# Self-attention projections: which batch stores the split weight slices, and when the first slices are loaded

## The chip, the core and the metric

The kernel runs on one core of a Trainium2 chip. The core has TensorE (PE, matrix products into PSUM; PEld is its loading of weights), VectorE (DVE), ScalarE (ACT), GpSimd (POOL) and SyncE (SP). SP issues most DMAs, ACT a few; both queues are served in order, so a DMA that must wait holds up all that stand behind it. The metric is the device time of one execution in microseconds (us). Several runs are taken and the median counts.

## What is computed

A decoder layer on four sequences (batches 0 to 3) of 1024 tokens with 512 features, followed by a gated fusion. Only the first third matters here, causal self-attention with 16 heads of 32 features:

```python
xn1 = _ln(x, g1, be1)
q = jnp.einsum('btc,hcd->bhtd', xn, Wq) + bq[None, :, None, :]
k = jnp.einsum('bsc,hcd->bhsd', kv_src, Wk) + bk[None, :, None, :]
v = jnp.einsum('bsc,hcd->bhsd', kv_src, Wv) + bv[None, :, None, :]
scores = jnp.einsum('bhtd,bhsd->bhts', q, k) / scale     # scale = DH ** (-0.5)
attn = jax.nn.softmax(jnp.where(mask, scores, -jnp.inf), axis=-1)
out = jnp.einsum('bhts,bhsd->bhtd', attn, v)
x = x + (sa @ W1 + b1)
...                       # cross-attention, feed-forward, gated fusion
```

The scores are large (divided by a number below 1), so products are made with more than one pass of PE: every operand is held as a high part and a low part (the rest after rounding), and three products are added, high x high, high x low, low x high.

## The kernel before, in words

**Phases.** `self_attention`, `cross_attention` and `feed_forward` follow one another. Only the first is touched.

**Units and pieces.** A batch has four head groups g (four heads, 128 features) and two token halves n of 512. A *piece* `project(b, n, g)` makes k and q of one group and half: two times twelve matmuls of 128x512 (`pk`, `pq`), each started by a step `load` that fetches the weight slice of 128 columns if n is 0. `values(b, n, half)` makes v for half of the features: four times twelve matmuls of 128x256 (`pv`), with a slice of 256 columns. `front(b, n)` loads four blocks of x (L524), normalises them (`stats_s`, `mv_s`, `rstd_s`, then L178), transposes them on PE (`tpn_s`, L534) and splits them into `xn` (L74 the high half on ACT, L75 the low one on DVE).

The results of k, q and v go to DRAM (L623 `kd<-k`, `qd<-q`; L594 `vd<-vout`) and come back rearranged as *stacks* of three parts (L646 `ks<-kd`, `qs<-qd`; L668 `v<-vd`). A *unit* u is one group and half of the query tiles; units are numbered through the batches. `maxima(u)` makes the scores of a unit (L692 `s<-ks,qs`), takes row maxima on DVE (L699 and L702, results `least` and `top`), transposes them (`tpm`) and writes them as extra rows of the query stack (L732 `qs<-mT`). `attend(u)` makes the scores again with that row included (L755 `st`), takes the exponential on ACT (L760), sums on POOL and DVE (L809) and multiplies with v (L785 `av`).

**Weight slices.** `weight_slice` is called for each slice (k and q: i = 0 to 3, v: i = 0 and 1) in each batch. In batch 0 it loads the raw slice into the one buffer `stage` (L577 `st_k`, `st_q`, `st_v`; 256 KB, v 512 KB), makes the high half on ACT (L578) and the low half on DVE (L579), and stores both halves to DRAM (L581 `wk<-wk`, 512 KB, v 1 MB). In batches 1 to 3 it loads the two halves from there (L569). Slices of k and q have four buffers, those of v one.

**What sets the order.** `run` merges streams of steps by their weights (main, ahead, fill); a timeline planner then orders the instructions of each engine at build time, by the cost it gives each of them. `tc.issue_after(i)` keeps what follows behind instruction i in that order; `behind(engine)` does so for the last instruction of an engine. `ones_rows` fills four rows of the key stacks by memsets on POOL (L510). While unit u is attended, the stream `ahead` holds the maxima of the next units, and `fill` the projections of unit u + 4.

Of the kernel before, what the change touches and what calls it, by code (L numbers as in the profile page):

```python
# [10 lines left out]
F32 = mybir.dt.float32  # L11
FR = mybir.dt.float32r
# [6 lines left out]
P = 128  # L19
B, T, C, H = 4, 1024, 512, 16  # L20
# [3 lines left out]
NC = C // P  # L24
NF = FF // P
TG = 512
# [20 lines left out]
def raw(ap):  # L47

    return ap.bitcast(F32)
# [3 lines left out]
def decoder_then_fusion(ctx: ExitStack, tc: tile.TileContext, x, ctxT, cols, rows,  # L53
                        Wq_s, Wk_s, Wv_s, W1, Wq_c, Wk_c, Wv_c, W2, Wf1, Wf2,
                        Wt, WvT, WgT, out):
    nc = tc.nc
# [34 lines left out]
    def product_steps(psum_of, a, b, a_at, b_at, width, end, bias=None):  # L91


        held = {}

        def step(c):
            if c == 0:
                held["ps"] = psum_of()
                if bias:
                    nc.tensor.matmul(held["ps"], *bias(), start=True, stop=False)  # L100
            for k, (i, j) in enumerate(((0, 0), (0, 1), (1, 0))):
                nc.tensor.matmul(held["ps"], a_at(a()[i], c), b_at(b()[j], c),  # L102
                                 start=not bias and c == 0 and k == 0, stop=c == NC - 1 and k == 2)
            if c == NC - 1:
                end(held["ps"])

        per = Z["per"]

        def steps(c):
            for i in range(c, c + per):  # L110
                step(i)

        return [(3 * width * per, lambda c=c: steps(c)) for c in range(0, NC, per)]
# [48 lines left out]
    latest = {}  # L162
# [290 lines left out]
    def self_attention(ph):  # L453
# [62 lines left out]
        def front(b, n):  # L516

            uid = f"s{b}_{n}"
            hs = []

            def load(j):
                i = n * NJ + j
                t = xp.tile([P, C], F32, tag="x", name=f"x_{b}_{i}")
                nc.sync.dma_start(t, x[b, i * P : (i + 1) * P, :])  # L524
                normalise(t, t, f"{uid}_{j}")
                hs.append(t)

            def turn(c):
                if c == 0:
                    xn[b, n] = [xnp.tile([P, NC, TG], FR, tag=f"xn{n}_{k}", name=f"xn{k}_{uid}") for k in range(2)]  # L530
                parts = xn[b, n]
                tp = psum(f"tpn_{uid}_{c}")
                for j, t in enumerate(hs):
                    nc.tensor.transpose(tp[:, j * P : (j + 1) * P], t[:, c * P : (c + 1) * P], ident)  # L534
                with tc.issue_after(latest["hi"]) if c and (b, n) in Z["chain"] else ExitStack():
                    nc.scalar.activation(tp, tp, AF.Identity, bias=col("be1", c), scale=col("g1", c))
                split(parts[0][:, c, :], parts[1][:, c, :], tp, f"{uid}_{c}")

            return [(0, lambda j=j: load(j)) for j in range(NJ)], [(TG, lambda c=c: turn(c)) for c in range(NC)]
# [19 lines left out]
            return slice(at[0] * P, (at[-1] + 1) * P), slice(first * P, (first + len(at)) * P)  # L559


        sources = {"k": (Wk_s, 1.0), "q": (Wq_s, -1.0), "v": (Wv_s, 1.0)}
        slices = {}

        def weight_slice(which, i, w):

            t = wp.tile([P, 2, NC, w], FR, tag=f"w{w}", name=f"w{which}_{i}", bufs=None if w == P else 1)
            if (which, i) in slices:
                nc.sync.dma_start(raw(t), slices[which, i])  # L569
                return t  # L570
            src, sign = sources[which]
            if Z["wst"]:
                st = wp.tile([P, 2 * TG], F32, tag="stage", name=f"st_{which}_{i}", bufs=Z["wst"])
            else:
                st = ptp.tile([P, 2, TG], F32, tag="pT", name=f"st_{which}_{i}").rearrange("p a b -> p (a b)")
            st = st[:, : NC * w].rearrange("p (c n) -> p c n", c=NC)
            nc.sync.dma_start(st, chunks(src)[:, :, i * w : (i + 1) * w])  # L577
            nc.scalar.activation(t[:, 0], st, AF.Copy, scale=sign)  # L578
            nc.vector.scalar_tensor_tensor(t[:, 1], st, sign, t[:, 0], ALU.mult, ALU.subtract)  # L579
            slices[which, i] = dram.tile([P, 2, NC, w], F32, tag=f"w{which}{i}", name=f"w{which}{i}")  # L580
            nc.sync.dma_start(slices[which, i], raw(t))  # L581
            return t

        ws = {}

        def values(b, n, half):
            def load():
                if n == 0:
                    ws["v"] = weight_slice("v", half, C // 2)

            def end(ps, j):
                v = outp.tile([P, C // 2], F32, tag="vout", name=f"vout_{b}_{n}_{half}_{j}")
                nc.scalar.copy(v, ps)
                nc.sync.dma_start(v_dram[b,][:, n * NJ + j, half * (C // 2) : (half + 1) * (C // 2)], v)  # L594

            steps = [(0, load)]
            for j in range(NJ):
                steps += product_steps(
                    lambda j=j: psum(f"pv_{b}_{n}_{half}_{j}")[:, : C // 2],
                    lambda: xn[b, n], lambda: [ws["v"][:, 0], ws["v"][:, 1]],  # L600
                    lambda a, c, j=j: a[:, c, j * P : (j + 1) * P], lambda w, c: w[:, c, :], C // 2,
                    lambda ps, j=j: end(ps, j))
            return steps

        def project(b, n, g):
            steps = []
            for which, to in (("k", k_dram), ("q", q_dram)):
                def load(which=which):
                    if n == 0:
                        ws[which, g] = weight_slice(which, g, P)  # L610

                def end(ps, which=which, to=to):
                    parts = [qkp.tile([P, TG], FR, tag=f"part{k}", name=f"{which}{k}_{b}_{n}_{g}")
                             for k in range(2)]
                    bias = col("bk_s", g) if which == "k" else nbq[:, g : g + 1]
                    split_biased(parts[0], parts[1], ps, bias)

                    moves = [(to[b, n, g], slice(0, TG), slice(0, TG))] if which == "k" else [
                        (to[b, h, g], *shared) for h, tiles in enumerate(tiles_of(b, g))
                        if (shared := columns(tiles, n))]  # L620
                    for dram_tile, at, src in moves:
                        for k in range(2):
                            nc.sync.dma_start(dram_tile[k][:, at], raw(parts[k])[:, src])  # L623

                steps.append((0, load))
                steps += product_steps(
                    lambda which=which: psum(f"p{which}_{b}_{n}_{g}"),
                    lambda which=which: [ws[which, g][:, 0], ws[which, g][:, 1]], lambda: xn[b, n],
                    lambda a, c: a[:, c, :], lambda a, c: a[:, c, :], TG, end)
            return steps  # L630
# [10 lines left out]
        def pile(stack, src, parts):  # L641

            for i, k in enumerate(parts):
                nc.sync.dma_start(raw(stack)[i * DH : (i + 1) * DH], src[k].rearrange("(r d) t -> d r t", d=DH))  # L646

        def load_stacks(u, since):

# [22 lines left out]
        def maxima(u):  # L672
# [12 lines left out]
            def scores(blocks):  # L685
# [3 lines left out]
                for r, j, m in blocks:  # L689
                    part = sc[:, at : at + width(tiles[j], m)]  # L690
                    at += width(tiles[j], m)
                    nc.tensor.matmul(part, q_at[u][:KS, r, j * P : (j + 1) * P],  # L692
                                     k_at[u, m][:KS, r, : part.shape[-1]], start=True, stop=True)
                    parts.append(part)
                for part, (r, j, m) in zip(parts, blocks):
                    far = tiles[j] >= NJ
# [159 lines left out]
        for b, g, n in [(b, g, n) for b in range(B) for g in range(NC) for n in range(NG)]:  # L856
            piece = project(b, n, g)
            if (g, n) == (0, 0):
                piece = ((among(piece, fronts[b, 1][1]) if Z["amt"] else fronts[b, 1][1] + piece) if b else
                         fronts[b, 0][0] + [(0, ones_rows)] + fronts[b, 0][1] + fronts[b, 1][0] + piece  # L860
                         + fronts[b, 1][1] + values(b, 0, 0))
            elif (g, n) in Z["val"]:
                piece = piece + values(b, *Z["val"][g, n])
            if b + 1 < B:
# [74 lines left out]
        for u in range(len(units)):  # L939
# [17 lines left out]
            if u >= first_late:  # L957
                fill, part = [], Z["late"][u - first_late] * total
                while rest and (part > 0 or u + 1 == len(units)):
                    part -= rest[0][0]  # L960
                    fill.append(rest.pop(0))
            else:
                fill = pieces[u + AHEAD]
            run(main, ahead, fill, speed=(Z["main"], (Z["ahead%d" % n] if u < Z["alf"] else Z["ahead_l"]) if u else Z["a0"], Z["fill"]), sooner=(Z["so0"], Z["so1"], Z["so2"]))
        first, others, end = tail()
        first()
# [840 lines left out]
```

## Time and profile before

| | |
|---|---|
| median of 3 runs | 2146.06 us (2144.63 to 2152.42) |
| profiled execution | 2153.24 us, span 2151.5 us |
| mean granted clock of PE | 0.983 |
| PE busy | 2064.3 us, 96% of the span |
| DVE, ACT, POOL busy | 1452.1 (67%), 967.5 (45%), 1210.7 us (56%) |
| moved by DMA | 379.36 MB, mean 176 GB/s |
| first weight slice loaded and split | 2.6 to 8.7 us |
| first scores (L692) | 37.2 us |
| self-attention | up to about 880 us |

The profile is that of one execution. In the tables of stretches each engine has its busy time and its number of instructions; PEclk is the clock that was granted to PE, as a share of the full one, and DMA share the mean busy share of the core's 16 DMA engines. A line "A <- B: t, n, m" of the waits says that A waited for B t us in n waits, the longest of m us. The chain of waits lists, in order of time, the start, the length and the name of each link of the chain that ended last; for a DMA this is from issue to landing. In a timeline, a line has start, busy time, engine, source line and operation, result and operand, and how many were merged.

### The profile page before, as it was taken

Reading aid. Unit: us, or ns where it says so; the run is one execution under the profiler, and the core shown is the slowest. Engines: PE = TensorE matmul, PEld = TensorE weight load, DVE = VectorE, ACT = ScalarE, POOL = GpSimd, SP = SyncE. Lnnn points to the kernel's source line nnn. Section 1 sums busy time; section 2 is a strip of 40 time slices with the busy share of each in tenths; the row PEclk is TensorE's granted clock in tenths of the full one; section 3 lists DMA queues with packets and bytes.
Section 4 is the critical chain, followed back from the end, with each engine's and each line's share of the span. In section 5 each row is a group of like instructions: output and inputs, shape, how many; then the busy total and the mean of one; then the engine's idle time right before and its main releaser. Section 6 shows DMA issues by size and latency. Waiting matters only on the chain.

```text
span 2151.5 us, 34750 instructions
## 1 busy us (share of the span) xinstructions
PE 2064.3 (96%) x11544; PEld 1568.7 (73%) x11544; DVE 1452.1 (67%) x3134; ACT 967.5 (45%) x2180; POOL 1210.7 (56%) x1257
## 2 busy tenths in 40 slices
PE   6999998999999989989999999999999999999997
PEld 5766676667667756457888887788788888888885
DVE  6587757665755587567676776877667846865667
ACT  3365555555565545435555557433322422232222
POOL 3288878888788877774555543512343524433323
PEclk9999999999999998999999999999999999999998
DMA  8866767677666567662323122965576457655631
GB/s 245 258 186 168 218 203 216 182 243 219 190 174 186 158 171 213 206 204 79 99 84 103 50 79 86 332 210 170 182 238 198 166 175 237 207 175 171 220 113 39
DMA packets 241321, 379.36 MB, mean 176 GB/s; under 512 B 35948, under 2 KB 104284, under 8 KB 239094
## 3 DMA queue, kind: packets, MB, share of 16 engines
q1 hardware_dynamic: 215532, 348.32, 52.4%
q10 hardware_dynamic: 25610, 28.83, 4.4%
q8 instruction: 92, 1.51, 0.3%
q14 instruction: 87, 0.71, 0.1%
HBM read 251.71 MB, written 124.81 MB: 175 GB/s over the span
## 4 chain that ended last, share of the span: by engine, by line
PE 76%; DMA 7%; DVE 7%; POOL 4%; issue 2%; ACT 1%; SPq 1%; ACTq 0%; DVEq 0%; POOLq 0%
PE acc L1495 15%; PE ph L1473 14%; PE st L755 5%; PE s L692 5%; PE av L785 5%; PE po_c L102 4%; PE pq_x L102 3%; PE pk L102 3%; PE pv L102 3%; PE pg_o L102 3%; PE po_x L102 3%; PE pq L102 3%; POOL pT L809 2%; PE sc_c L87 2%; PE av_c L1139 1%
## 5 line engine op out<-in xcount | busy, mean ns | idle before, releaser
L809 POOL TENSOR_TENSOR pT<-pT,pT 128x256 f32<-128x256 f32 (+3 forms) x369 | 551.6, 1514 | 106.0 <-PE av L785 97.1
L760 ACT ACTIVATE pT<-st 128x512 f32<-128x512 f32 (+2 forms) x640 | 322.3, 559 | 171.2 <-PE st L755 122.9
L1495 PE MATMUL acc<-wf,hs 128*128 128x512 f32 x1536 | 392.1, 393 | 0.9 <-DVE y L1507 0.9
L1495 PEld LDWEIGHTS acc<-wf,hs 128*128 128x128 f32 x1536 | 285.8, 188 | 63.1 <-ACT inT L74 1.3
L699 DVE CUSTOM_DVE_ANT_0 s<-s,mask 128x128 f32<-128x128 f32 (+3 forms) x512 | 244.5, 504 | 99.6 <-PE s L692 97.1
L692 PE MATMUL s<-ks,qs 96*128 96x512 f32 (+3 forms) x768 | 230.2, 371 | 23.0 <-DMA qs<-qd 7.3
L702 DVE TENSOR_REDUCE top<-s 128x1 f32<-128x512 f32 x256 | 171.9, 684 | 104.4 <-PE s L692 103.9
L755 PE MATMUL st<-qs,ks 98*128 98x256 f32 (+2 forms) x888 | 227.8, 340 | 4.7 <-ACT pT L760 2.0
L1473 PE MATMUL ph<-inT,wp 128*128 128x512 f32 x768 | 205.3, 396 | 3.1 <-DVE p L1431 1.2
L755 PEld LDWEIGHTS st<-qs,ks 98*128 98x128 f32 x888 | 149.4, 192 | 63.7 <-issue 20.2
L692 PEld LDWEIGHTS s<-ks,qs 96*128 96x128 f32 x768 | 135.6, 194 | 81.0 <-issue 17.0
L1473 PEld LDWEIGHTS ph<-inT,wp 128*128 128x128 f32 x768 | 143.9, 189 | 36.6 <-DVE gp_o L1568 1.8
L785 PE MATMUL av<-pT,v 128*32 128x512 f32 (+3 forms) x1776 | 155.1, 454 | 4.1 <-POOL pT L768 4.1
L1473 PE MATMUL ph<-inX,wp 128*128 128x512 f32 x576 | 151.4, 395 | 1.1 <-DVE inX L75 1.1
L768 POOL TENSOR_SCALAR_AFFINE_SELECT pT<-pT 128x256 f32<-128x256 f32 x256 | 103.7, 421 | 73.6 <-ACT pT L760 73.1
L1473 PEld LDWEIGHTS ph<-inX,wp 128*128 128x128 f32 x576 | 108.4, 189 | 25.2 <-issue 1.3
L1542 POOL TENSOR_TENSOR y<-y,row_bf 128x512 f32<-128x512 f32 x32 | 41.6, 1304 | 132.6 <-DMA y<-x 72.1
L1481 ACT ACTIVATE hs<-ph 128x512 fp32r<-128x512 f32 x64 | 38.3, 599 | 172.2 <-DVE ph L1431 99.4
L102 PE MATMUL pk<-xn_s,wk 128*128 128x512 f32 x384 | 106.1, 412 | 4.9 <-DVE top L702 3.0
L102 PE MATMUL pv<-wv,xn_s 128*128 128x256 f32 x768 | 108.1, 286 | 2.5 <-DVE least L699 1.6
L102 PEld LDWEIGHTS pv<-wv,xn_s 128*128 128x128 f32 x768 | 102.1, 192 | 11.4 <-DVE top L699 2.9
L1118 POOL TENSOR_TENSOR p_c<-p_c,inv_c 128x512 f32<-128x512 f32 x64 | 68.4, 1069 | 73.9 <-DVE inv_c L1117 58.6
(262 smaller groups left out, 3907.8 us busy)
## 6 DMA issues: line engine op xcount, KB each, us to landing
wp<-wpd SPq DMA_DIRECT2D x168, 256.0 KB
ks<-kd SPq DMA_DIRECT2D x96, 256.0 KB
qs<-qd SPq DMA_DIRECT2D x96, 256.0 KB
wf<-w2fd SPq DMA_DIRECT2D x48, 512.0 KB
kd<-k SPq DMA_DIRECT2D x64, 256.0 KB
qd<-q SPq DMA_DIRECT2D x120, 128.0 KB
wpd<-wp SPq DMA_DIRECT2D x56, 256.0 KB
x<-in_x SPq DMA_DIRECT2D x32, 256.0 KB
```

The source lines that it names most:

```text
L102: nc.tensor.matmul(held["ps"], a_at(a()[i], c), b_at(b()[j], c), start=not bias and c == 0 and k == 0, stop=c == NC - 1 and k == 2)
L692: nc.tensor.matmul(part, q_at[u][:KS, r, j * P : (j + 1) * P], k_at[u, m][:KS, r, : part.shape[-1]], start=True, stop=True)
L699: nc.vector.tensor_tensor_reduce(part, part, mask[:, TG - part.shape[-1] :], 1.0, TOP, ALU.add, ALU.min, dst)
L702: nc.vector.tensor_reduce(dst, part, AX.X, ALU.min)
L755: nc.tensor.matmul(st[:, i], k_at[u, kb // NJ][:KM, r + i, (kb % NJ) * P : (kb % NJ + 1) * P], q_at[u][:KM, r + i, c0:], start=True, stop= ...
L760: nc.scalar.activation(held[kb][(r + i) // 2][:, at : at + k, c0:], st[:, i : i + k], AF.Exp, scale=-QSCALE)
L768: nc.gpsimd.affine_select(out=t, in_=t, compare_op=ALU.is_ge, fill=0.0, base=0, pattern=[[0, 2], [1, P]], channel_multiplier=-1)
L785: return nc.tensor.matmul(held["av"][r * DH : (r + 1) * DH, c0:], v_at[b, g][:, kb, r * DH : (r + 1) * DH], held[kb][r // 2][:, r % 2, c0: ...
L809: eng.tensor_tensor(t[:, :, c0:], t[:, :, c0:], p[:, :, c0:], ALU.add)
L1118: nc.gpsimd.tensor_tensor(pr, pr, inv.unsqueeze(2).to_broadcast([P, HH, S]), ALU.mult)
L1473: nc.tensor.matmul(ps, w[:, q, c], x[:, r, c], start=c == 0 and m == 0, stop=c == HC - 1 and m == 2)
L1495: mm = nc.tensor.matmul(accs[j], hidden[b, n, f][:, q, j * P : (j + 1) * P], w2s[b, f][:, r], start=begins and m == 0, stop=ends and m == 2)
```

## The change

- Slices are made per batch. In batch 0 they are split and not stored. In batch 1 (`b == True` holds for b = 1, as `LATER` names all slices) the raw slices are loaded and split once more and stored. Batches 2 and 3 load the stored halves as before.
- The first slices of k and q of batch 0 are loaded into two free `pT` buffers (2 of the 7 that hold exponentials later), by steps that come right after the first four loads of x. All other raw slices share the one `stage` buffer, as before.
- The memsets of `ones_rows` come after the loads and the normalisation of the second half.
- Batch 1's loads of x wait, in SP's order, for the last instruction that SP has been given so far.
- The score matmuls of unit 1 wait, in PE's order, for the latest projection matmul; and during unit 0 the stream `ahead` begins with an empty step of weight 4 x 512.

```diff
@@ product_steps @@
             for k, (i, j) in enumerate(((0, 0), (0, 1), (1, 0))):
-                nc.tensor.matmul(held["ps"], a_at(a()[i], c), b_at(b()[j], c),
-                                 start=not bias and c == 0 and k == 0, stop=c == NC - 1 and k == 2)
+                latest["product"] = nc.tensor.matmul(
+                    held["ps"], a_at(a()[i], c), b_at(b()[j], c),
+                    start=not bias and c == 0 and k == 0, stop=c == NC - 1 and k == 2).ins
@@ front @@
-                nc.sync.dma_start(t, x[b, i * P : (i + 1) * P, :])
+                with behind(nc.sync) if b == 1 else ExitStack():
+                    nc.sync.dma_start(t, x[b, i * P : (i + 1) * P, :])
@@ slices @@
+        LATER = [(w, i) for w in 'kqv' for i in range(NC)]
+        FIRST = ((0, 0, "k"), (0, 0, "q"))
+
+        def first_slices():
+            def load(which):
+                ws[which, 0] = weight_slice(0, which, 0, P)
+            return [(0, lambda which=which: load(which)) for _, _, which in FIRST]
+
-        def weight_slice(which, i, w):
+        def weight_slice(b, which, i, w):
...
-            if Z["wst"]:
-                st = wp.tile([P, 2 * TG], F32, tag="stage", name=f"st_{which}_{i}", bufs=Z["wst"])
+            if (b, i, which) not in FIRST:
+                st = wp.tile([P, 2 * TG], F32, tag="stage", name=f"st_{which}_{b}_{i}", bufs=1)
             else:
                 st = ptp.tile([P, 2, TG], F32, tag="pT", name=f"st_{which}_{i}").rearrange("p a b -> p (a b)")
...
-            slices[which, i] = dram.tile([P, 2, NC, w], F32, tag=f"w{which}{i}", name=f"w{which}{i}")
-            nc.sync.dma_start(slices[which, i], raw(t))
+            if b == ((which, i) in LATER):
+                slices[which, i] = dram.tile([P, 2, NC, w], F32, tag=f"w{which}{i}", name=f"w{which}{i}")
+                nc.sync.dma_start(slices[which, i], raw(t))
@@ values, project @@
-                    ws["v"] = weight_slice("v", half, C // 2)
+                    ws["v"] = weight_slice(b, "v", half, C // 2)
-                    if n == 0:
-                        ws[which, g] = weight_slice(which, g, P)
+                    if n == 0 and (b, g) != (0, 0):
+                        ws[which, g] = weight_slice(b, which, g, P)
@@ maxima @@
+        def among_fill():
+            return tc.issue_after(latest["product"])
...
-                    nc.tensor.matmul(part, q_at[u][:KS, r, j * P : (j + 1) * P],
-                                     k_at[u, m][:KS, r, : part.shape[-1]], start=True, stop=True)
+                    with among_fill() if u == 1 else ExitStack():
+                        nc.tensor.matmul(part, q_at[u][:KS, r, j * P : (j + 1) * P],
+                                         k_at[u, m][:KS, r, : part.shape[-1]], start=True, stop=True)
@@ the pieces of (g, n) == (0, 0), batch 0 @@
-                         fronts[b, 0][0] + [(0, ones_rows)] + fronts[b, 0][1] + fronts[b, 1][0] + piece
-                         + fronts[b, 1][1] + values(b, 0, 0))
+                         fronts[b, 0][0] + first_slices() + fronts[b, 0][1] + fronts[b, 1][0]
+                         + [(0, ones_rows)] + piece + fronts[b, 1][1] + values(b, 0, 0))
@@ the loop over units @@
+            if u == 0:
+                ahead.insert(0, (4 * TG, lambda: None))
             run(main, ahead, fill, ...)
```

The names and line numbers in the prediction are those of the kernel before.

More of the change, by code (lines that the diff above doesn't have):

```diff
@@ L559, in columns @@
             return slice(at[0] * P, (at[-1] + 1) * P), slice(first * P, (first + len(at)) * P)
+        LATER = [(w, i) for w in 'kqv' for i in range(NC)]
         sources = {"k": (Wk_s, 1.0), "q": (Wq_s, -1.0), "v": (Wv_s, 1.0)}
         slices = {}
-        def weight_slice(which, i, w):
-            t = wp.tile([P, 2, NC, w], FR, tag=f"w{w}", name=f"w{which}_{i}", bufs=None if w == P else 1)
+        FIRST = ((0, 0, "k"), (0, 0, "q"))
[4 more added lines that the diff above has]
+        def weight_slice(b, which, i, w):
+            t = wp.tile([P, 2, NC, w], FR, tag=f"w{w}", name=f"w{which}_{b}_{i}", bufs=None if w == P else 1)
             if (which, i) in slices:
```

## The prediction

> **What bounds the kernel now.** I began with the table of busy time by stretch, cut where the orders of instructions of the two kernels differ: every engine's order has changed from the start until about 645 us, and from there on it is the same.
>
> ```profile
> core 0: us, PE busy (x) PEld busy (x) DVE busy (x) ACT busy (x) POOL busy (x), PEclk, DMA share, GB/s
> 0.00:67.00 67.00, 47.75 (x226) 37.77 (x227) 40.89 (x100) 22.33 (x38) 20.20 (x41) 0.92 0.78 237
> ...
> 100.00:180.00 80.00, 77.59 (x507) 52.68 (x506) 66.15 (x169) 47.12 (x94) 61.59 (x62) 1.00 0.69 195
> 180.00:340.00 160.00, 156.53 (x1071) 112.51 (x1070) 101.32 (x305) 89.34 (x179) 132.82 (x135) 1.00 0.70 201
> 340.00:400.00 60.00, 54.40 (x347) 38.06 (x345) 37.70 (x108) 32.20 (x64) 46.71 (x52) 0.91 0.56 169
> ```
>
> PE sets the pace: 97% busy from 100 to 340 us. Time can be won only where it stands or is slow, and that is the opening: 19.25 of the first 67 us idle, at a mean clock of 0.92, with the DMA engines at 78% (99% from 20 to 40 us). Next, what PE waited for up to 160 us (total, times, longest):
>
> ```profile
> PE tpn_s L534 <- DVE x L178: 8.4, 3, 6.8
> PE s L692 <- DMA qs<-qd: 5.1, 2, 3.1
> PE s L692 <- DVE top L702: 1.7, 2, 0.9
> PE pv L102 <- DVE least L699: 1.6, 1, 1.6
> PE tpm L726 <- DVE least L699: 1.4, 1, 1.4
> ```
>
> The first line is the wait for the first activations (6.8 at the start), which the change leaves. The rest is stack loads and VectorE's score maxima. The chain of waits dates them:
>
> ```profile
> 28.93 8.26 DMA qs<-qd
> 37.23 0.55 PE s L692 x2
> 37.78 2.41 PE pk L102 x6
> ...
> 48.26 7.93 DMA qs<-qd
> ...
> 57.19 4.92 PE pk L102 x12
> ```
>
> Each stack load of 256 KB takes 8 us to land, PE stands before both (1.94 and 3.13 us), and the projection after each runs at about half speed: 0.40 us a matmul, against 0.23 for the twelve at 92.96 (2.75 us). Last, SP's queue between 25 and 33 us, in order:
>
> ```profile
> 25.33 0.34 SPq L581 DMA_DIRECT2D wv<-wv  x1
> 25.76 0.38 SPq L646 DMA_DIRECT2D ks<-kd  x1
> 26.19 3.55 SPq L646 DMA_DIRECT2D qs<-qd  x3
> 29.78 0.51 SPq L594 DMA_DIRECT2D vd<-vout  x1
> 30.33 0.49 SPq L577 DMA_DIRECT2D st_k<-in_Wk_s  x1
> 30.92 2.00 SPq L524 DMA_DIRECT2D x<-in_x  x2
> ```
>
> A store of 1 MB (wv) goes out just ahead of the stacks that PE waits for, and batch 1's activations just after.
>
> **The change, part by part.** *Stores removed from batch 0:* eight of 512 KB and two of 1 MB, 6 MB. *In batch 1* ten loads of split slices (6 MB) become ten raw loads (3 MB) with a split each and ten stores (6 MB). The splits are 8 x 0.63 + 2 x 1.06 = 7.2 us more on ACT and 8 x 0.69 + 2 x 1.22 = 8.0 on DVE. *Moved:* the raw loads of the first k, q and v slices go ahead of x_4; those of k 1, q 1 and v 1 ahead of the first k and q stores; batch 1's four x loads and their statistics from 31-50 us to behind unit 1's loads, which the new order puts at 110-170 us; four memsets of POOL (1.8 us each, 9.6 to 16.9) behind the second half's rstd; unit 1's first scores behind twelve matmuls of pk_0_1.
>
> I follow PE by landmarks.
>
> *Start of the projections: loses 1.5 us, 0 to 2.6.* DVE's first low half (13.64) gets wv's split and two statistics more ahead of it: 1.22 + 2 x 0.69 = 2.6. Against that, x_2 and x_3 took 2.11 us together beside the memsets, where x_0 and x_1 took 0.5 each; with the memsets gone, 1.0 comes back.
>
> *First scores: 2.5 us earlier, start included; -3 to +4.* Slices of k 1, q 1 and v 1 share one stage buffer, so each load waits on SP for the split before it, and the stores of the first k and q are queued behind all three; ACT's copy of k, too, stands behind q 1's split. From 13.5 us (wv split) two rounds of load, ACT and DVE follow. A raw load took 3.5 us (103.49) to 7.7 (30.33, in the crowd); I take 4, since little else is in flight: 13.5 + 2 x (4 + 1.3) = 24.1, where kd goes out at 21.88 now. So the store is 2.2 us later. But 17.8 to 37.2 us carries 4736 KB now and 3456 KB afterwards (no wq and wv stores, a q load instead); 1.3 MB at 295 GB/s are 4.4 us. The stacks land at about 34.5 instead of 37.23. With 7.7 us a load they land after 40.
>
> *First scores to the maxima's transpose (37.2 to 52.9): 3 us, 1.5 to 4.5.* DVE loses four statistics and four normalisations of batch 1 (4 x (0.69 + 0.17 + 0.55) = 5.6) and two splits here. PE's three waits for it (1.63, 0.45, 1.44) mostly go, and the six slow matmuls (2.41 against 1.38) are warm.
>
> *Unit 1's scores: 4 us, 2 to 5.3.* Their stacks get no wk, wq or x traffic beside them, but two vout stores stand ahead of qs on SP. The 3.13 us wait is covered by pk_0_1 (2.75 us), which needs only k 1, long split. Its cold clock costs 4.92 - 2.75 = 2.17 now. All is 5.3; I keep 1.3 for a late vout.
>
> By 67 us that is 9.5. *67 to 100 us: 0.5 more, -1 to 2:* the waits of 0.83 and 0.91 on `top` are unit 1's and stay. *100 to 180 us: 2.5 us lost, 0 to 6.* Batch 1's normalising (5.6) and three of its splits (1.22 + 2 x 0.69 = 2.6) come in, two of batch 0's (1.4) leave; DVE rises from 66.15 to 73 of 80 us, and its results free the score banks. PE stands 2.4 us here now; I let that double. *Batch 1's slices: nothing, -3 to 4.* Their first use is at 175.8 us, and the split loads go out from 107 us on. The cover is these 60 us, against 4 + 1.3 a slice; each store waits on SP for DVE, and the stack loads are behind it. If the cover is gone, see the third rival.
>
> Sum: 2.5 + 3 + 4 + 0.5 - 2.5 = 7.5 us. The profiled execution took 2153.24 us (span 2151.5 and 1.7 around it), 7.2 above the median of the runs; it would take 2145.7, and the median goes to 2146.06 - 7.5 = **2138.5**.
>
> The row for the clock is 0.40 us a matmul after 1.94 us of waiting. [...]
>
> **Rivals.** *No change, +5 to -3 us:* the opening is won but DVE takes it back from 100 to 180 us (6 instead of 2.5) and the raw loads take 7.7 us. For it: DVE is at 17.9 and 18.8 of 20 us in 120-140 and 160-180. Against it: it is at 60% from 67 to 100, and slips are made up there.
>
> *More, 13 to 24 us off:* the stretch 340 to 400 us has 5.6 us of PE idle and 0.09 x 60 = 5.4 us of slow clock, from one stack load (338.26, 6.22 us) and DVE at 19.25 of 20 us (360-380). If the new order misses this collision, half to all of the 11 comes on top. Against it: the same batch 2 loads meet there.
>
> *Slower, 11 to 30 us:* SP in batch 1. Each of ten stores waits there for its split on DVE; a store of a split waited 4.7 us once (L581 on mv_s), and k, q and stack moves are queued behind. A stall like that at 344 us cost PE 2.28 idle and 4.34 - 2.75 = 1.6 of clock, 3.9. It decides from the fifth of the ten on: 5 x 3.9 - 7.5 = 12; all ten give 31. Against it: SP already waits for work of other engines and PE stays at 98% (180-340).
>
> *That it doesn't do what it says* can be left out: the orders show no slice store in batch 0 and ten in batch 1.
>
> **How the numbers follow.** Forecast (3 to 13 us off) 0.50; no change 0.19; more 0.18; slower 0.13. Half a per cent, about what a measurement here can tell from none, is 10.7 us. Faster: the 0.18 and a third of the forecast, 0.35; slower 0.13; the rest 0.52. The range runs from 22 us off, inside "more", to 5 on, and leaves out the slower case: 2124 to 2151.
>
> **What would show it.** Right: the first scores start at 34-36 us and the first after the transpose without a DMA wait; the clock of the first 67 us is above 0.96; PE's `top` and `least` waits grow in 100-180; the lead, taken at pk_0_2, is about 10 us. Wrong: kd first issued after 28 us (raw loads slow), a lead that is gone by 180 us (DVE), or waits of SP for slice splits with PE idle behind them between 180 and 340.

## The result: 20 us slower, and the profile after

The changed kernel took 2170.79 us (median of 5 runs, 2166.95 to 2177.88), the kernel before 2152.25 us in runs taken beside it (2144.63 to 2153.02). The ratio over the rounds is 1.0095, with an interval of 1.0076 to 1.0114; that is some 20 us. The forecast of 2138.5 and its range of 2124 to 2151 were wrong, and the rival with the chance of 0.13 came nearest. The profiled execution took 2177.88 us, with a span of 2176.2 against 2151.5 and a mean clock of 0.981 against 0.983. It is the slowest of the five, so the steps read from it below may be larger than in a usual execution.

In the changed kernel the names are at other lines: raw loads L589, high halves L590, splits (low halves on VectorE) L591, stores of slices L594, `s` L710, `least` L717, `top` L720, `tpm` L744, `st` L773, additions of weights L827. The same stretches as in the prediction:

```profile
core 0: us, PE busy (x) PEld busy (x) DVE busy (x) ACT busy (x) POOL busy (x), PEclk, DMA share, GB/s
0.00:67.00 67.00, 51.38 (x276) 41.21 (x277) 41.30 (x102) 27.94 (x49) 20.31 (x40) 1.00 0.75 212
...
100.00:180.00 80.00, 74.25 (x447) 47.54 (x446) 63.29 (x160) 45.90 (x88) 60.05 (x61) 0.94 0.59 171
180.00:340.00 160.00, 140.50 (x925) 98.62 (x924) 111.12 (x271) 75.42 (x152) 116.01 (x123) 0.94 0.61 178
```

The opening is better, as forecast: 3.6 us more PE work in 67 us, at a clock of 1.00 instead of 0.92. From 180 to 340 us, where PE had been 156.53 us busy at full clock, it is 140.50 us busy at 0.94. To date it, take the first `mT<-tpm` instruction of each unit, in both timelines. The changed kernel leads by 3.3 us at unit 0 (49.95 against 53.23) and by 5.1 at unit 1 (90.71 against 95.85). It lags by 4.5 at unit 4 (181.98 against 177.52) and still by 4.5 at unit 6. Unit 7 lags by 13.8, unit 8 by 15.8, unit 9 by 29.6 (333.69 against 304.05). From unit 12 to 27 the lag stays at 26.3 to 26.7 us. So two steps, of 9.3 and 13.8 us, make the result. PE's waits from 160 to 345 us name them:

```profile
PE tpm L744 <- DVE least L741: 8.2, 1, 8.2
PE pv L102 <- DVE least L717: 8.0, 2, 7.6
PE s L710 <- DVE top L720: 0.9, 1, 0.9
```

In the kernel before, the longest waits of the same stretch are short and for DMAs:

```profile
PE s L692 <- DMA kd<-k: 2.3, 1, 2.3
PE st L755 <- DMA qs<-mT: 1.4, 1, 1.4
```

In the changed kernel PE doesn't wait for weights or stacks there but, twice, for VectorE. VectorE's timeline (start, busy time, line, operation) at the two places:

```profile
258.43 9.98 DVE L591 SCALAR_TENSOR_TENSOR wk<-st_k,wk 128x512 fp32r<-128x512 f32 x1 [1.86 <-ACT wk L590]
268.33 1.27 DVE L720 TENSOR_REDUCE top<-s 128x1 f32<-128x512 f32 x2
...
297.01 9.37 DVE L591 SCALAR_TENSOR_TENSOR wq<-st_q,wq 128x512 fp32r<-128x512 f32 x1 [0.59 <-ACT wq L590]
306.30 0.55 DVE L717 CUSTOM_DVE_ANT_0 s<-s,mask 128x384 f32<-128x384 f32 x1
```

A split that takes 0.69 us elsewhere took 9.98 (the third k slice of batch 1) and 9.37 (the fourth q slice). The maxima behind it on VectorE came late, the score banks stayed full, and PE stood. GpSimd's timeline beside the first:

```profile
256.15 3.63 POOL L827 TENSOR_TENSOR pT<-pT,pT 128x768 f32<-128x768 f32 x2
259.74 0.41 POOL L786 TENSOR_SCALAR_AFFINE_SELECT pT<-pT 128x256 f32<-128x256 f32 x1
260.11 1.29 POOL L827 TENSOR_TENSOR pT<-pT,pT 128x512 f32<-128x512 f32 x1
261.36 0.40 POOL L786 TENSOR_SCALAR_AFFINE_SELECT pT<-pT 128x256 f32<-128x256 f32 x1
261.73 6.13 POOL L827 TENSOR_TENSOR pT<-pT,pT 128x512 f32<-128x512 f32 x5
277.35 1.29 POOL L271 TENSOR_TENSOR w_l<-w_l,w_h 128x512 fp32r<-128x512 f32 x1 [9.48 <-ACT w_h L270]
```

GpSimd works without a gap until 261.73 + 6.13 = 267.86 and then stands. The split ends at 258.43 + 9.98 = 268.41, 0.55 us later. The second one ends at 306.38, 0.56 us after GpSimd's last addition (305.82). It looks as if each split waited for GpSimd and then needed its own half microsecond; the experiments test this. To the 8 us of standing comes the clock behind it, in steps of 5 us:

```profile
260.00:265.00 5.00, 1.52 (x9) 1.16 (x7) 5.00 (x1) 1.03 (x2) 5.00 (x6) 1.00 0.00 0
265.00:270.00 5.00, 0.26 (x2) 0.26 (x2) 5.00 (x5) 0.00 (x0) 2.86 (x3) 0.53 0.16 61
270.00:275.00 5.00, 5.00 (x32) 2.47 (x31) 3.73 (x13) 1.60 (x3) 0.00 (x0) 0.50 0.96 266
```

The first row shows VectorE "busy" for 5.00 us with one instruction. In the last, PE works again, at half speed, and loses 2.5 us more.

### The profile page after: what moved, and what is told of

It reads as the page before. It is cut to its first block, busy times and chain, and to the rows that moved or that the text cites. A ratio compares the mean times of both kernels' runs of the same rounds, so it can differ in the third digit from the quotient of the medians.

```text
span 2176.2 us, 34763 instructions
## 1 busy us (share of the span) xinstructions
PE 2071.1 (95%) x11544; PEld 1570.0 (72%) x11544; DVE 1475.7 (68%) x3144; ACT 972.2 (45%) x2190; POOL 1212.4 (56%) x1257
## 4 chain that ended last, share of the span: by engine, by line
PE 76%; DVE 9%; DMA 7%; POOL 3%; issue 3%; ACT 1%; SPq 1%; DVEq 0%; ACTq 0%; POOLq 0%
PE acc L1516 15%; PE ph L1494 14%; PE s L710 5%; PE av L803 5%; PE st L773 5%; PE pq_x L102 4%; PE po_c L102 4%; PE pv L102 4%; PE pg_o L102 3%; PE pq L102 3%; PE po_x L102 3%; PE pk L102 3%; PE sc_c L87 2%; POOL pT L827 2%; PE av_c L1160 1%
## 5 line engine op out<-in xcount | busy, mean ns | idle before, releaser
L827 POOL TENSOR_TENSOR pT<-pT,pT 128x256 f32<-128x256 f32 (+3 forms) x369 | 549.3, 1507 | 115.8 <-PE av L803 107.5
L717 DVE CUSTOM_DVE_ANT_0 s<-s,mask 128x128 f32<-128x128 f32 (+3 forms) x512 | 244.2, 503 | 93.7 <-PE s L710 91.1
L710 PE MATMUL s<-ks,qs 96*128 96x512 f32 (+3 forms) x768 | 232.9, 375 | 23.3 <-DVE top L720 6.2
L720 DVE TENSOR_REDUCE top<-s 128x1 f32<-128x512 f32 x256 | 171.7, 684 | 91.9 <-PE s L710 90.9
L773 PE MATMUL st<-qs,ks 98*128 98x256 f32 (+2 forms) x888 | 226.2, 340 | 6.2 <-DMA qs<-mT 4.5
L710 PEld LDWEIGHTS s<-ks,qs 96*128 96x128 f32 x768 | 136.4, 194 | 84.6 <-DVE top L720 18.9
L773 PEld LDWEIGHTS st<-qs,ks 98*128 98x128 f32 x888 | 150.5, 193 | 63.6 <-ACT pT L778 20.6
L102 PE MATMUL pv<-wv,xn_s 128*128 128x256 f32 x768 | 113.3, 296 | 10.0 <-DVE least L717 8.0
```

The lines of the kernel that those rows point to most:

```text
L102: latest["product"] = nc.tensor.matmul(held["ps"], a_at(a()[i], c), b_at(b()[j], c), start=not bias and c == 0 and k == 0, stop=c == NC - ...
L717: nc.vector.tensor_tensor_reduce(part, part, mask[:, TG - part.shape[-1] :], 1.0, TOP, ALU.add, ALU.min, dst)
L720: nc.vector.tensor_reduce(dst, part, AX.X, ALU.min)
L773: nc.tensor.matmul(st[:, i], k_at[u, kb // NJ][:KM, r + i, (kb % NJ) * P : (kb % NJ + 1) * P], q_at[u][:KM, r + i, c0:], start=True, stop= ...
L827: eng.tensor_tensor(t[:, :, c0:], t[:, :, c0:], p[:, :, c0:], ALU.add)
```

## The experiments

Ratios are to the kernel before, from five rounds, in brackets the 95% interval. "Lag" is how much later than in the profile of before the `mT` instruction of unit 27 is (765.43 us there), read from each kernel's profiled execution. That is one execution, and not always a typical one: it is the slowest of the runs in the changed kernel, the fastest in e4, and 7 us above the median in e8.

| kernel | ratio | lag, us | longest split in batch 1, us |
|---|---|---|---|
| the changed kernel | 1.0095 [1.0076, 1.0114] | 26.3 | 9.98, 9.37 |
| e1_store_first | 1.0024 [1.0010, 1.0038] | 5.7 | none made |
| e2_split_second | 1.0127 [1.0099, 1.0154] | 32.1 | 10.20, 9.29 |
| e3_pool | 1.0054 [1.0036, 1.0072] | 19.2 | none on VectorE |
| e4_one_input | 1.0029 [1.0014, 1.0044] | 7.5 | 0.69 (v 1.22) |
| e5_x_free | 0.9998 [0.9984, 1.0011] | -5.5 | none made |
| e6_scores_free | 1.0028 [1.0015, 1.0040] | 6.4 | none made |
| e7_first_only | 0.9987 [0.9971, 1.0003] | 0.9 | none made |
| e8_two_first | 1.0060 [1.0038, 1.0083] | 19.3 | 9.51 |
| e9_split_x_free | 1.0127 [1.0106, 1.0148] | 29.6 | 10.19, 9.84 |
| e10_one_input_x_free | 1.0024 [1.0013, 1.0035] | 9.1 | 0.69 (v 1.22) |
| e11_half_first | 1.0021 [1.0008, 1.0033] | 6.9 | 1.64 |
| e12_pool_waits | 1.0063 [1.0043, 1.0083] | 5.9 | 2.92 |
| e13_pool_light | 1.0038 [1.0024, 1.0053] | 11.7 | 2.31 |
| e14_light_store_first | 1.0090 [1.0074, 1.0106] | 10.4 | none made |

### Which part of the change costs

**e1_store_first**: batch 0 stores, batch 1 loads.

```diff
-        LATER = [(w, i) for w in 'kqv' for i in range(NC)]
+        LATER = []
```

> The changed kernel, but batch 0 stores its ten split slices again and batches 1 to 3 load them; the earlier first loads and all the reordering stay. Three theories of the 25 us that the changed kernel loses to the kernel before. Stretched splits (A): two of the ten splits of batch 1 on VectorE took 9.98 and 9.37 us in place of 0.69, each ending within 0.6 us of the end of an unbroken run of GpSimd instructions; with no splits in batch 1 both vanish and the 3 to 5 us of lead that the trace shows at 50 to 91 us are left: ratio to the kernel before 0.996 to 0.999. SyncE (B): the stores of batch 1 wait in SyncE's queue for their splits and hold the k, q and stack moves behind them; the same ratio here. Order (C): the reordering of the opening loses it, the splits cost only their own 0.7 us each: 1.007 to 1.010, as the changed kernel.

1.0024: splitting in batch 1, with its loads and stores, accounts for most of the loss, which is against C. It is also slower than A and B said. The lead of 3.9 us at unit 1 was lost again by unit 7.

**e2_split_second**: the changed kernel with `FIRST = ()`, the `ones_rows` step where it was, and without `among_fill`, the empty step and `behind(nc.sync)`. Only the splitting and storing in batch 1 is left.

> The kernel before with one part of the change alone: batch 0 does not store, batch 1 loads, splits and stores again; no earlier first loads, no reordering. A: slower, by as much as its splits happen to meet GpSimd's runs, 1.003 to 1.013, with at least one split of batch 1 over 3 us long that ends within 0.6 us of the end of a run of GpSimd instructions. B: 1.008 to 1.012, without such a split, and TensorE waiting for stacks. C: 0.998 to 1.002.

1.0127, with the two splits of the same two slices stretched again:

```profile
L591 DVE SCALAR_TENSOR_TENSOR wk<-st_k,wk x2: 694/5446/10197, 262.1 to 289.7; 128x512 fp32r<-128x512 f32 x2
L591 DVE SCALAR_TENSOR_TENSOR wq<-st_q,wq x2: 691/4991/9291, 277.9 to 301.2; 128x512 fp32r<-128x512 f32 x2
```

(Shortest, median and longest in ns, from 240 to 312 us.) This part alone is no faster than the whole change, so the reordering of the opening is not what costs. A gave this size and the stretched splits; B's range ended at 1.012, without such splits.

### What stretches a split

**e3_pool**: batch 1's low halves on GpSimd.

```diff
+            if b:
+                if sign != 1.0:
+                    nc.scalar.mul(st, st, sign)
+                nc.scalar.copy(t[:, 0], st)
+                nc.gpsimd.tensor_tensor(t[:, 1], st, raw(t[:, 0]), ALU.subtract)
+            else:
```

> The changed kernel, but the low halves of batch 1's slices are subtracted on GpSimd in place of VectorE (for q after one more ScalarE pass that turns the sign). A: no VectorE instruction is stretched to 9 us, and the waits of 8.2 and 7.6 us of TensorE on VectorE go; GpSimd carries ten more instructions of 1.3 to 2.6 us: 0.998 to 1.002. B: the stores still wait in SyncE's queue, now for a split behind GpSimd's longer queue: 1.008 or slower. C: 1.007 to 1.010.

1.0054, between the theories. The waits for VectorE of 8 us are gone, and the lag is 5.5 us at unit 9, but it grows to 16.2 by unit 11, with new waits of PE (160 to 380 us):

```profile
PE s L716 <- DMA v<-vd: 4.2, 1, 4.2
PE s L716 <- DMA qs<-qd: 4.0, 1, 4.0
```

These are stack loads. They fit B, with the stores in SyncE's queue now waiting for a longer GpSimd; the runs don't show that link by itself.

**e4_one_input**: the sharpest test. The VectorE instruction stays, with its place and its store, but reads one operand.

```diff
-            nc.scalar.activation(t[:, 0], st, AF.Copy, scale=sign)
-            nc.vector.scalar_tensor_tensor(t[:, 1], st, sign, t[:, 0], ALU.mult, ALU.subtract)
+            if b:
+                nc.scalar.activation(t[:, 0], st, AF.Copy, scale=sign - 1.0)
+                nc.vector.tensor_reduce(t[:, 1], st.unsqueeze(3), mybir.AxisListType.X, ALU.max)
```

> The changed kernel, but in batch 1 the VectorE instruction that makes the low half reads one input only: a reduction over a length of one that copies the raw slice, as long (0.69 us) as the split, on the same engine, with the same store behind it. ScalarE writes what makes the two halves sum to the weight, so the weights of batches 1 to 3 keep one rounded part only. A: reductions of 128x512 took 0.69 us in every instance of the trace, also beside a busy GpSimd, so none is stretched and both long waits go: 0.997 to 1.001. If VectorE's time for ten more instructions, the stores in SyncE's queue (B) or the order (C) is the cause, nothing changes: 1.007 to 1.010.

1.0029, 14 us less than the changed kernel, and none is stretched:

```profile
L592 DVE TENSOR_REDUCE wk<-st_k x4: 673/681/686, 111.2 to 269.9; 128x512 fp32r<-128x512 f32 x4
L592 DVE TENSOR_REDUCE wq<-st_q x4: 683/686/686, 132.4 to 276.6; 128x512 fp32r<-128x512 f32 x4
```

The reduction of the third k slice began at 255.73 us, in the middle of an unbroken run of GpSimd (251.18 to 268.93 us), and took 0.69 us. All loads, stores and VectorE instructions of batch 1 are there, so B, C and VectorE's added time are not what costs these 14 us. With one operand in SBUF the stretch did not come. The ratio is above A's 1.001: A is right on the mechanism and left a remainder.

**e8_two_first**: the two stretched slices are stored in batch 0 (`LATER` without `('k', 2)` and `('q', 3)`).

> The changed kernel, but the two slices whose splits were stretched to 9.98 and 9.37 us (the third k and the fourth q) are stored in batch 0 and loaded in batch 1; the other eight are split and stored in batch 1 as in the changed kernel. If the two stretched splits are the loss, 14 to 20 us go and the rest stays: 1.001 to 1.004, as with one input. If they had only stood where something else waited, or other splits fall on GpSimd's runs in their place: 1.006 to 1.010.

1.0060, the case of "other splits in their place". With the third k slice gone, the third q slice's split came at 261.21 us, was held for 9.51 us, and ended 0.54 us after GpSimd's run. The other stretch is gone. It is the moment, not the slice. The runs lie wide apart (2154.21 to 2174.46 us, the profiled one 2171.32), so the hold may not come in every execution.

**e12_pool_waits**: GpSimd reads one column of each split's result in batch 1.

```diff
+            if b:
+                seen = outp.tile([P, 1], F32, tag="seen", name=f"seen_{which}_{b}_{i}", bufs=1)
+                nc.gpsimd.tensor_scalar(seen, raw(t[:, 1])[:, 0, :1], 1.0, 0.0, ALU.mult, ALU.add)
```

> The changed kernel with nothing taken away; behind each split of batch 1 one small GpSimd instruction is added that reads one element a partition of the split's result, so that GpSimd's queue stands still at that point until VectorE has made its split. If the splits are held by GpSimd's unbroken runs, they are done soon after GpSimd reaches that instruction: none longer than 4 us, the TensorE waits of 8 us gone, 1.002 to 1.006 (what is left after one input in place of two was 1.0029, and GpSimd now stands still a little). If a split is slow for a reason of its own (its place, its tile, the store behind it), it stays at 9 to 10 us and GpSimd's standing still comes on top: 1.010 or more.

No split over 2.92 us in the profile, but not for the reason expected: the third k split (255.74 us, 0.93 us) was over before GpSimd came to the new instruction (258.71). It came 2.7 us earlier than in the changed kernel and got in between two of GpSimd's additions (4.07 us together, 3.63 in the changed kernel). The ratio of 1.0063 is from runs that lie wide apart (2155.24 to 2175.62, the profiled one 2159.36), so it may differ between executions. Not conclusive on the mechanism.

**e13_pool_light** and **e14_light_store_first**: half of GpSimd's additions left out in units 4 to 9; e14 with `LATER = []` as well.

```diff
                     for i, (t, p) in enumerate(zip(held[0], held[kb])):
+                        if 4 <= u < 10 and i:
+                            continue
```

> The changed kernel with half of GpSimd's additions of weights left out in units 4 to 9 (the second of the two halves, so the row sums of two heads of each are too small there): GpSimd's runs around the two stretched splits are about half as long, the splits keep both inputs. If GpSimd's unbroken runs hold the splits: none over 5 us, the two TensorE waits of 8 us gone or halved, 1.000 to 1.005. If GpSimd has nothing to do with it: two splits of 9 to 10 us as before, 1.008 to 1.010.

1.0038, and the splits from 240 us on, both operands in SBUF, are short:

```profile
L591 DVE SCALAR_TENSOR_TENSOR wk<-st_k,wk x2: 686/690/693, 263.0 to 280.3; 128x512 fp32r<-128x512 f32 x2
L591 DVE SCALAR_TENSOR_TENSOR wq<-st_q,wq x2: 692/752/812, 268.4 to 288.2; 128x512 fp32r<-128x512 f32 x2
```

The splits at 263.02 and 268.37 us began while GpSimd stood still, so this run shows what a split costs without a running GpSimd instruction, and not what half a run costs. With e4 it shows both halves of the cause here: two operands on VectorE, and GpSimd's work beside them.

> The same half of the additions left out, but batch 0 stores its slices and batch 1 splits nothing. Its time shows what a lighter GpSimd is worth without the splits: against 1.0024 of the first experiment 0.998 to 1.003. The difference between the run before this one and this is the cost of ten splits, loads and stores in batch 1 that are not held for long: 0 to 0.003 if only their own 7.6 us of VectorE count, more if they are still held.

A miss: 1.0090, slower than e13 with its splits. At unit 27 the lag is 10.4 us, and the span is 19.9 longer than before, so half of it arises after self-attention. The cause was not found, and the splits' own cost can't be had from this pair.

### The rest: the opening's lead, and the x loads

> The kernel of the first experiment (batch 0 stores, all else as in the changed kernel; ratio 1.0024 to the kernel before), with the second batch's x loads issued where the scheduler puts them again, not in the written order of SyncE's queue. Its trace had a lead of 3.9 us at unit 1 and a lag of 6.3 us from unit 7 on. Theory X: the x loads that now stand behind the moves of k, q and the stacks make batch 1's first block late: 0.996 to 0.999. Theory M: the scores of unit 1 that wait for the product before them, and the delay before unit 0's ahead work, lose it: 1.001 to 1.004. Theory N: neither; each edit moves waits of 1 to 3 us about, each of them followed by some us at half the granted clock: 1.001 to 1.004 whatever is undone.

> The kernel of the first experiment, with the scores of unit 1 no longer tied to the product before them and without the delay of unit 0's ahead work; the x loads stay in SyncE's written order. X: 1.001 to 1.004. M: 0.996 to 0.999. N: 1.001 to 1.004.

> The kernel of the first experiment with both undone: what is left of the change is the earlier loads of the first k and q slices and the later memset of the rows of ones. X, M: 0.996 to 0.999, as the prediction's first terms (first scores 2.5 us earlier, then 3 us) make 0.997. N: 1.000 to 1.004.

Against e1, **e5** drops `behind(nc.sync)`, **e6** drops `among_fill` and the empty step, **e7** both. 0.9998, 1.0028 and 0.9987: the order of the x loads is worth 0.0026 here, a little less than X said, and the scores of unit 1 nothing, against M. The first four x loads of batch 1 go out between 30 and 39 us in the kernel before and in e5, but between 102 and 117 us in the changed kernel and in e1, in the stretch where VectorE is fullest (63.29 of the 80 us from 100 to 180 in the changed kernel). What is left in e7 cannot be told from no change.

> The changed kernel, whole, but for the second batch's x loads, which the scheduler places again. Earlier runs: the changed kernel 1.0095, the stretched splits some 0.0066 of that (one input in place of two: 1.0029), the order of the x loads some 0.0026 (1.0024 with it, 0.9998 without it, both without splits in batch 1). If the two costs add: 1.005 to 1.008. If the x loads only move the stretched splits to other places, or take them off GpSimd's runs: 1.000 to 1.003, or as the changed kernel.

> The kernel with one input in batch 1 (a copy in place of the split; the weights of batches 1 to 3 keep one rounded part), and the x loads placed by the scheduler: both costs taken away, all loads and stores of the change kept. If the two are all of the loss: 0.998 to 1.001; the prediction's gain without its mis-sized terms would be 0.9965. If the stores and loads of batch 1 cost something of their own: 1.002 or more.

**e9** is the changed kernel and **e10** is e4, each without `behind(nc.sync)`. 1.0127 and 1.0024: the costs don't add. In e9 the stretched splits are at the same places, and the x loads gained nothing (1.0095 with the order); against e4's 1.0029, e10 is the same. So the 0.0026 belongs to e1's order and is no price of the x loads as such. An own cost of short splits is possible (e10 against e5: 1.0024 and 0.9998), but e4 against e1 shows none.

**e11_half_first**: only the first five slices of batch 1 are split there (`LATER` with k and q of two groups and v's first half), x loads free.

> A version that could beat both: the x loads placed by the scheduler; of the ten slices the first five that batch 1 splits (v's first half, k and q of the first two groups) stay unstored in batch 0, the other five, among them the two that were stretched, are stored in batch 0 as in the kernel before. If only splits between 247 and 306 us meet long runs of GpSimd: 0.997 to 1.000. If the splits between 104 and 177 us, one of them 2.29 us long, cost as well: 1.001 to 1.004.

1.0021, the case in which the earlier splits cost as well, and no split over 1.64 us. No version that splits in batch 1 beats the kernel before, and e5 and e7, which don't, can't be told from it.

## Why the prediction was wrong

**The step that failed is "Batch 1's slices: nothing, -3 to 4".** It measured 23.1 us (9.3 + 13.8) in the profiled execution; in the ratios, e4 and e1 are 14 and 15 us faster than the changed kernel. The other 13 us of the miss, from the forecast's ratio of 0.9965 to e1's 1.0024, are lost without any split in batch 1; the terms further below account for them as far as the traces show. The cover I named held: no wait of PE for a slice is among its waits from 160 to 345 us. The price was wrong. 0.69 us a split came from rows of batch 0, most of them made beside an idle GpSimd, while the table of stretches that I showed has GpSimd at 132.82 of 160 us where the splits went. The trace had rows to warn me: one split of 1.23 us beside GpSimd (79.46 us), and additions on VectorE of up to 3.40 us beside GpSimd's (129.69). I even used the normalising slowed by memsets in the opening and didn't carry it to batch 1. I misread that row, too: the 2.11 us at 9.56 are x_3's alone (x_2 took 0.54 us, before the memsets), so they cost 1.6 us there and not 1.0.

**The slower rival** had place and sign: ten splits of batch 1, PE idle between 180 and 340 us. Its mechanism was wrong. It had stalls of 3.9 us on SyncE's queue, deciding from the fifth on; it was two stalls of 9.3 and 13.8 on VectorE. SyncE did stand, by its own waits from 245 to 270 us:

```profile
SPq L594 <- DVE wk L591: 13.6, 1, 13.6
```

A stack load of q and four moves of the next q were queued behind that store (269.67 and 270.22 us), and SyncE issued nothing from 254.75 to 268.44 us.

But PE's waits name VectorE, and e4 keeps the stores without the stalls.

**First scores, 2.5 us forecast: nothing.** The chain of the changed kernel:

```profile
29.17 7.40 DMA qs<-qd
36.57 0.74 issue
37.31 0.52 PE s L710 x2
37.83 1.40 PE pk L102 x6
```

The k store went out at 24.47 us (24.1 forecast, 21.88 before), but the scores began at 37.31 against 37.23. From that store to the scores it took 12.84 us instead of 15.35, and the later store used up these 2.5 us. I had turned 1.3 MB less traffic into 4.4 us at 295 GB/s. The traffic did fall (185 GB/s from 20 to 40 us, DMA share 0.67 against 0.99), but much of that was before the stacks: from 20 to 24 us, while the raw loads came one by one, the share was 0.18. While the last stack load was under way the DMA engines were as full as before (1.01 against 1.05; a packet counts in the stretch where it begins) at 228 GB/s instead of 289, and it took 7.40 us instead of 8.26.

**First scores to the transpose, 3 us: right** (3.3 at unit 0), with the projection warm as said (six matmuls in 1.40 us). **Unit 1's scores, 4 us, and 67 to 100, 0.5: too much.** The lead grew by 1.9 by unit 1, not 4.5. The wait before those scores is 2.06 us (3.13 before), and a new one came at 77.7 us, 3.2 us on `top`. There VectorE had stood for 3.32 us until the last raw q slice of batch 0 was ready to split (76.40 us): its load went out only at 70.32 us, when the split before it (to 69.71) had freed the single `stage` buffer.

**100 to 180 us, 2.5 lost: 9.6 lost** (from 5.1 ahead at unit 1 to 4.5 behind at unit 4; 7.4 of it by unit 2). PE's standing was as I said: 5.75 us, double the 2.41 before. What I left out is the clock: 0.94 over 80 us is 4.8 us. I priced it behind the stalls of the opening and not behind new ones. Waits of 1.42 us (to 118.35), 2.34 (to 155.34) and 3.16 (to 77.74) left such stretches (0.50 from 120 to 124, from 157 to 159 and from 78 to 84 us), but those of 1.19, 1.39 and 2.06 us from 36 to 54 us did not (1.00 from 36 to 60 us), so the length of the wait alone doesn't decide it. The shortest of those that the half clock followed, 1.42 us, is below the 1.94 us of the prediction's row. The wait of 1.42 us came right behind a split again: the first k split of batch 1 took 2.29 us (115.60 to 117.89) beside an addition of GpSimd, and the maxima that PE waited for were next on VectorE.

**"More"** did not happen: the collision of batch 2 stays, and the lag shrinks by about 1 us from unit 10 (27.5) to 13 (26.4). **"No change"** described 100 to 180 us, but not what came after.

## What to carry to other kernels

A duration is the price of an instruction beside the neighbour that it had (here a split took 0.69 us, and 9.98 beside GpSimd's run): before moving VectorE work with two SBUF operands, read GpSimd's busy column in the stretch where it lands, and how long GpSimd's unbroken runs are there. What queues behind that instruction counts too; here it was the score maxima that free PE's banks (waits of PE of 8.2 and 7.6 us). A new wait of PE can bring the half clock behind it (here one of 1.42 us did, one of 2.06 us did not), so price it at least as a risk. Don't turn bytes saved into time at a fixed rate: see first whether they moved in the very stretch where the transfer on the path waits.

## What the runs showed of the hardware

Seven splits, VectorE instructions with two SBUF operands, were held until GpSimd's whole run was over: for 8.6 to 9.5 us over their own time, in four kernels (the changed one, e2, e8, e9), and all ended 0.54 to 0.56 us after GpSimd's last instruction. Another 28 splits of k and q, in 14 of the kernels, took 0.74 to 2.94 us, and each of these, too, ended 0.54 to 0.56 us after an instruction of GpSimd had ended: they were let in at a boundary between two of its instructions (e12 at 255.74 with 0.93 us, e9 at 131.49 with 1.64 us). GpSimd's instruction behind such a boundary took longer, too: an affine select 0.86 us instead of 0.41 in e9 (132.54 us), a step of `rstd_s` 1.00 us instead of 0.55 in the changed kernel (117.30 us). Why some boundaries let VectorE in and, in these seven cases, at least six in a row did not (in the changed kernel nine and eight instructions of GpSimd ended during the two holds), stays open. A memset of GpSimd, which reads nothing, held no split (0.67 us at 21.25 in the changed kernel, inside a memset of 2.09). Reductions with one operand of 128x512 never were longer than 0.69 us: 340 of the score maxima, which read PSUM, ran wholly beside a busy GpSimd in the traces of before and after, and 13 of the 16 reductions of k and q slices in e4 and e10, which read SBUF, met one.
